# Two layers of cross attention and routed experts: the second attention's first batches prepared by groups, and new waits for gathers and scatters

## The chip, the cores and the metric

The kernel runs on one core of a Trainium2 chip. All data is float32. The metric is the device time of one execution in microseconds (us); the median of several executions is compared.

The core has five engines that run side by side, each with its own queue of instructions, worked off in order: TensorE (PE in the profile) multiplies matrices into PSUM banks, with its weight loads listed apart as PEld; VectorE (DVE) and ScalarE (ACT) work elementwise on SBUF and PSUM; GpSimd (POOL) works elementwise on SBUF and starts gathers and scatters by index; SyncE (SP) starts all other DMA transfers. An engine that needs another's result waits on a semaphore.

## The reference

The input x has 64 batches of 128 rows of 128 numbers. Each of two layers adds a cross attention and then a feed-forward part with two experts per row:

```python
x = x + xattn0(layernorm(x), fside, ctx, ctx)       # 16 heads of 8; keys: 128 made + 120 given
x = x + ffn0(layernorm(x))                          # each row: the best 2 of 8 experts, F = 352, gated
x = x + xattn1(layernorm(x), ctx, ctx)              # 16 heads of 8; 120 keys
x = x + ffn1(layernorm(x))                          # each row: the best 2 of 8 experts, R = 64, gelu
```

An attention is q = norm(x) Wq + bq, k = ctx Wk + bk, v = ctx Wv + bv, softmax(q k / sqrt(8)) v for each head, then Wo and bo. In ffn0 a row that chose experts e1 and e2 gets share1 * ffn(e1) + share2 * ffn(e2).

## The kernel before

The batches go in 16 groups of four (`GB = 4`); the rows of a group stay in SBUF in `xg[g]` from beginning to end. The kernel has three stages in time.

**First attention** (`attention(0, ...)`), with the first router inside it. The router chooses two experts for every row and scatters each row twice to the array `xs` in HBM, into places sorted by expert (L783, 128 scatters on GpSimd). Each scatter may overtake others, but is made to wait for the one four places before it (`DEEP = 4`, helper `behind`).

**Tile stage** (`tile_stage`): 71 tiles of 256 rows of one expert each. Tiles 0 to 31 (`NA = 32`) hold rows of the first ten groups' batches, the others the rest. Per tile: SyncE fetches rows, weights and shares (`fetch`, L1051, L1058), TensorE turns the rows (L1075), multiplies into the hidden layer (L1085, with ScalarE's L1089 and VectorE's L1090) and projects back (L1098); VectorE multiplies by the share (L1104) and SyncE writes 256 rows to the array `ys` in HBM (L1105). After tile t, `between(t)` runs some of the other work. A part of that is `first_results(t)`: for pairs of batches u = 0 to 3, starting at tile NA + 9 + 8u, in five steps at successive tiles: GpSimd gathers the rows of batches 2u and 2u + 1 from `ys` (four gathers, L1127), adds them to x (two additions, L1139), VectorE takes mean and variance (L112, L113), and after every second pair GpSimd makes the normed rows of a group (roots L155, rows L167, kept in `READY`) and adds a bias. So the normed rows of groups 0 and 1 are there when the stage ends. Keys and values of group 0 for the second attention are also made between tiles (L202, L214).

**Second attention** (`attention(1, ...)`, `first` false), with the second layer's feed-forward as `Aside1` inside it. Iteration `it` works on several batches at different steps. In the written order of one iteration: values of batch it - 3 (L446, copied by ScalarE L455); a round in which TensorE makes for batch `it` the products whose maximum VectorE takes (L373, L385), and for batch it - 2 the scores whose exponential ScalarE takes (L401, L409); a piece of the expert feed-forward; `prep(it, 0)`; the output steps of older batches (L475, L462, L482); router work; `prep(it, 1)`; `shift` for batch it - 1, which turns the maxima (L430) and adds them to the queries (VectorE L433).

Before a batch can take its L373 its queries must be there. For a whole group that is four steps: four turns of normed rows into one bank (`turned`, L176), one copy to SBUF `xnT` (ScalarE L177), one product with Wq 512 columns wide (L289), and four query pieces `q4` (ScalarE L293, each 512 wide). For group 0 the kernel before does it batch by batch instead (`prep_batch`): one turn (L313), one copy (L314), one product 128 wide (L316), four pieces 128 wide (L318), called once ahead of iteration 0 and then in iterations 0, 1 and 2. Group 1's four steps stand at the end of iteration 3 (L577 to L581), its keys (`prep_k`, L202, ScalarE L207) in iteration 1 and its values (`prep_v`, L214, VectorE L221) in iteration 2. Later groups are prepared by `prep`, spread over four iterations.

The order of TensorE, ScalarE, VectorE and GpSimd is that of the program text (`manual_schedule` with `ORDERED`); for SyncE a scheduler decides in most of the kernel. Waits are derived from what instructions read and write. Tiles come from pools: a tile of the same tag takes turns over `bufs` places, and a pool opened after another is closed takes over its memory. The second attention's work pool lies where the tile stage's had been, so the first users of its tiles wait for what used that memory: the tile stage's last instructions and its DMA transfers from or to it.

Two kinds of edits of waits occur in the code. `declare_no_dep(ins, group=...)` tells that an instruction doesn't conflict with those of a group, so no wait is derived between them. `behind(ins, earlier)` adds waits by hand. With them the gathers of `first_results` are declared free of the writes of tiles 32 on, and then put behind `needed`, the writes of tiles 32 to 39 + 8u.

Of the kernel before, what the change touches and what calls it, by code (L numbers as in the profile page):

```python
# [44 lines left out]
def transformer_kernel(ctx, tc, a, out):  # L45
# [186 lines left out]
    def attention(layer, w, norm, first, aside):  # L232
# [5 lines left out]
        with ExitStack() as es:  # L238
# [84 lines left out]
            def prep(it, half):  # L323

                g, j = it // GB + 1, it % GB
                if not first:
                    if g == 1:
                        if (j, half) == (2, 1):
                            prep_v(1)
                        elif (j, half) == (1, 0):  # L330
                            prep_k(1)
                    elif g < NG:
                        pieces = (
                            (), (lambda: prep_k(g),),
                            (lambda: prep_v(g), lambda: prep_x(g)),
                            (lambda: prep_q(g, 0), lambda: prep_q(g, 1)),
                        )[j]
                        if half < len(pieces):
                            pieces[half]()
# [172 lines left out]
            else:  # L512
                prep_batch(0)
                loads(1)
            oTs, pos_ = {}, {}

            for it in range(B + 5):
# [13 lines left out]
                if first and it % GB == 2:  # L531
                    norm_of(it // GB + 2)
                if 2 <= it <= B + 1:
                    ps_[it - 2] = work.tile([128, nc_, 4, 512], F32, name="p", tag="p")
# [23 lines left out]
                else:  # L558
# [4 lines left out]
                    aside.piece(mtile)  # L563
                    if it < GB - 1:
                        prep_batch(it + 1)
                    prep(it, 0)
# [8 lines left out]
                    if it > GB and it % GB == 1:  # L575
                        norm_of(it // GB + 1)
                    if it == GB - 1:  # L577
                        normed[1] = READY[1]
                        prep_x(1)
                        prep_q(1, 0)  # L580
                        prep_q(1, 1)  # L581
                    aside.fetch_for(it)
# [184 lines left out]

    AFTER = mybir.DependencyInfo(mybir.DependencyClass.Sync, mybir.DependencyReason.DATA)
    DEEP = 4
    scatters, spare = [], []  # L770

    def behind(ins, earlier):
        for e in earlier:
            tc.add_manual_dep(ins.ins, e.ins.name, AFTER, reason="rows of one array")

    def scatter(probe, j, k, xn):
# [9 lines left out]
        if scatters:  # L786
            tc.declare_no_dep(s.ins, group="scatters", reason="rows of their own")
        behind(s, [scatters[-DEEP] if len(scatters) >= DEEP else spare[0]])
        tc.add_to_no_dep_group("scatters", s.ins)
# [232 lines left out]
    def tile_stage(work, mtile):  # L1022
# [14 lines left out]
        def fetch(t):  # L1037
# [9 lines left out]
            share = s[:, n + 3 * TT : n + 3 * TT + 2].rearrange("p (h d) -> p h d", h=2)  # L1047
            first_ = scatters[2 * GA * GB - DEEP : 2 * GA * GB]
            assert len(first_) == DEEP
            for dst, src in ((x, xs[bass.ds(r, TT), :D]), (share, xs[bass.ds(r, TT), bass.ds(e + D, 1)])):  # L1050
                f = nc.sync.dma_start(dst, src.rearrange("(h p) d -> p h d", p=S))  # L1051
                if t < NA:

                    tc.declare_no_dep(f.ins, group="scatters", reason="rows of the first groups")
                    behind(f, first_)
                    tc.add_to_no_dep_group("scatters", f.ins)
# [56 lines left out]
        def first_results(t):  # L1113
# [6 lines left out]
            if step == 0:  # L1120
# [4 lines left out]
                for b in range(2):  # L1125
                    for k in range(2):
# [3 lines left out]
                        )  # L1130
                        tc.declare_no_dep(g.ins, group="writes", reason="other tiles")
                        behind(g, needed)
                        groups.add("reads")
# [172 lines left out]
    class Aside1:  # L1306


        def __init__(self, pool):
            self.pool, self.got, self.b, self.xn = pool, {}, 2 * GB, READY[0]  # L1310
            self.xnTs, self.gates, self.ready = {}, [], []
# [22 lines left out]
        def lead(self, b):  # L1334
# [7 lines left out]
            if b % GB == GB - 1:  # L1342
                norms[2].roots(b + 1 - GB, b + 1)

        def normed(self, j):

            return self.xn

# [183 lines left out]
```

## Time and profile before

| | |
|---|---|
| median of 3 runs | 1597.97 us (1597.46 to 1599.05) |
| the profiled execution | 1601.67 us |
| its span from first to last instruction | 1599.9 us |
| TensorE busy | 1484.9 us, 93% |
| VectorE busy | 1084.0 us, 68% |
| ScalarE busy | 843.9 us, 53% |
| GpSimd busy | 641.1 us, 40% |
| mean granted clock of TensorE | 0.959 of full |
| second attention begins | at about 988 us of the span |

A profile row of the timeline gives the start in the span, the duration, the engine, the line of the code, the operation, the tile written and the tiles read, shapes, and a count where several equal instructions are put together. In brackets stands how long the engine had been idle before and what ended the wait. A float32 product appears as two matmul instructions (L289, one product, is "x2"), a turn (L176, L313) as one. A row of the table of windows gives for a stretch of time how busy each engine was, then the clock that TensorE was granted (1.00 is full speed), the share in which DMA engines were busy, and GB/s moved. The chain of work is followed back from the last instruction through what each waited for.

### The profile page before, as it was taken

To read this page: it belongs to the slowest core of one execution; us is meant where nothing else is said; L and a number is where in the kernel's file an instruction comes from. 1 tells how busy PE (TensorE), PEld (TensorE's weight loads), DVE (VectorE), ACT (ScalarE), POOL (GpSimd) and SP (SyncE) were. 2 spreads that over 40 slices of the span, in tenths; PEclk is the share of its full clock that TensorE was granted. 3 is DMA by queue.
4 is the path that set the end of the run, shared out by engine and by line. 5 is a ranking of instruction groups with operands and counts; after the bars stand their busy time and mean duration, and the time that the engine had idled before them with its cause. 6 is when DMAs were issued, how large, how long until landed. Compare 5 with 4: busy or idle time off the path is not lost.

```text
span 1599.9 us, 45004 instructions
## 1 busy us (share of the span) xinstructions
PE 1484.9 (93%) x18162; PEld 1182.0 (74%) x18162; DVE 1084.0 (68%) x2960; ACT 843.9 (53%) x1739; POOL 641.1 (40%) x1195
## 2 busy tenths in 40 slices
PE   7989999999999999888999998988999999999987
PEld 5767777777777777777888887767777777777765
DVE  6757888888888986454744443677666666667753
ACT  4646666666666655432333333666555555555643
POOL 4122255555565535443020302366554544443210
PEclk9999999999999999999999999799999989999999
DMA  8842122222222221466776664110111100000000
GB/s 218 228 115 59 48 57 56 62 60 60 60 60 59 53 71 44 133 190 186 202 212 193 201 186 127 30 32 21 37 31 29 31 29 28 27 27 15 15 8 27
DMA packets 143586, 133.22 MB, mean 83 GB/s; under 512 B 48402, under 2 KB 125970, under 8 KB 141458
## 3 DMA queue, kind: packets, MB, share of 16 engines
q1 hardware_dynamic: 135186, 113.02, 25.7%
q0 software_dynamic: 8192, 17.32, 3.5%
q8 instruction: 144, 2.36, 0.6%
q14 instruction: 64, 0.52, 0.1%
HBM read 97.31 MB, written 32.97 MB: 81 GB/s over the span
## 4 chain that ended last, share of the span: by engine, by line
PE 73%; DVE 10%; DMA 4%; issue 3%; SPq 3%; POOL 3%; ACT 3%; another core or an unknown queue 0%; POOLq 0%; ACTq 0%; DVEq 0%
PE bank L401 12%; PE bank L373 12%; PE bank L446 9%; PE bank L1085 9%; PE bank L1413 4%; PE bank L1392 4%; PE bank L1098 3%; DVE nm L385 3%; PE bank L289 2%; SPq L1247 2%; PE bank L1402 2%; PE bank L482 2%; DMA q<-xs 2%; PE bank L214 2%; PE bank L652 2%
## 5 line engine op out<-in xcount | busy, mean ns | idle before, releaser
L385 DVE TENSOR_REDUCE nm<-bank 128x2 f32<-128x496 f32 (+1 forms) x768 | 465.9, 664 | 141.3 <-PE bank L401 69.5
L401 PE MATMUL bank<-q,k 32*120 32x256 f32 (+1 forms) x3072 | 478.0, 408 | 16.4 <-DVE nm L385 5.0
L409 ACT ACTIVATE p<-bank 120x512 f32<-120x512 f32 (+1 forms) x768 | 403.3, 605 | 140.5 <-PE bank L401 106.0
L373 PE MATMUL bank<-k,q 32*128 32x248 f32 (+1 forms) x4096 | 462.4, 345 | 13.3 <-DMA k<-in_ctx_k 7.1
L373 PEld LDWEIGHTS bank<-k,q 32*128 32x128 f32 x4096 | 351.8, 191 | 81.6 <-issue 36.3
L401 PEld LDWEIGHTS bank<-q,k 32*120 32x120 f32 (+1 forms) x3072 | 302.0, 182 | 45.9 <-DVE nm L385 16.0
L446 PE MATMUL bank<-p,v 128*32 128x128 f32 (+1 forms) x4096 | 179.3, 279 | 4.6 <-DVE nm L385 3.9
L1090 DVE TENSOR_TENSOR p<-p,bank 128x256 f32<-128x256 f32 x213 | 87.8, 420 | 125.3 <-ACT p L1089 106.9
L155 POOL TENSOR_SCALAR rstd<-mv 128x4 f32<-128x4 f32 x32 | 6.3, 198 | 384.9 <-DVE mv L113 296.4
L783 POOL DMA_INDIRECT xs<-xn,at x128 | 129.4, 1011 | 28.5 <-issue 24.9
L455 ACT COPY ov<-bank 128x256 f32<-128x256 f32 x128 | 47.9, 375 | 170.5 <-PE bank L446 141.3
L1089 ACT ACTIVATE p<-bank 128x256 f32<-128x256 f32 x213 | 80.8, 385 | 102.4 <-PE bank L1085 92.4
L446 PEld LDWEIGHTS bank<-p,v 128*32 128x32 f32 (+1 forms) x4096 | 111.4, 111 | 29.6 <-issue 13.0
L1085 PE MATMUL bank<-q 128*128 128x256 f32 x516 | 122.4, 388 | 4.4 <-ACT oT L477 4.4
L433 DVE SCALAR_TENSOR_TENSOR q<-bank,c_smask,q 128x256 f32<-128x256 f32 x256 | 111.4, 477 | 12.7 <-PE bank L430 11.9
L1328 POOL DMA_INDIRECT yb<-ys,back x112 | 108.8, 971 | 27.7 <-issue 20.1
L167 POOL TENSOR_SCALAR xn<-x,mv,rstd 128x128 f32<-128x128 f32 x252 | 110.2, 447 | 7.5 <-issue 1.4
L293 ACT ACTIVATE q<-bank,c_a_bq,c_hmask 128x512 f32<-128x512 f32 x120 | 87.4, 787 | 45.3 <-PE bank L289 45.2
L1085 PEld LDWEIGHTS bank<-q 128*128 128x128 f32 x516 | 97.5, 196 | 17.0 <-ACT oT L477 4.8
L446 PE MATMUL bank<-p,vc 120*32 120x128 f32 x2048 | 104.2, 272 | 0.6 <-issue 0.5
L138 POOL TENSOR_TENSOR mv<-st 128x4 f32<-128x4 f32 x31 | 6.4, 206 | 205.4 <-DVE st L109 205.4
L1085 PE MATMUL bank<-vc 128*128 128x256 f32 x336 | 77.2, 379 | 0.0
(220 smaller groups left out, 2364.5 us busy)
## 6 DMA issues: line engine op xcount, KB each, us to landing
q<-in_w SPq DMA_DIRECT2D x43, 576.0 KB
vc<-in_w SPq DMA_DIRECT2D x28, 576.0 KB
vc<-in_ctx_v SPq DMA_DIRECT2D x16, 960.0 KB
ys<-zero SPq DMA_DIRECT2D x71, 128.0 KB
k<-in_ctx_k SPq DMA_DIRECT2D x32, 240.0 KB
q<-xs SPq DMA_DIRECT2D x43, 128.0 KB
ys<-q SPq DMA_DIRECT2D x43, 128.0 KB
x<-in_x SPq DMA_DIRECT2D x16, 256.0 KB
```

The costliest lines, as they stand in the source:

```text
L167: nc.gpsimd.tensor_scalar(xn[:, j, :D], xg[g][:, j, :], self.mv[:, b, 0:1], self.rstd[:, b : b + 1], ALU.add, ALU.mult,)
L293: nc.scalar.activation(q4s[g][:, :, s, :], pq.rearrange("p (b q) -> p b q", b=GB), AF.Identity, bias=w["bq"][:, s : s + 1], scale=hmask[:, ...
L373: nc.tensor.matmul(pa[:, u, :], lhsT=q4s[g][r, j, s, :], rhs=k2[g % 2][r, s // 2, j, :], start=True, stop=True,)
L385: nc.vector.tensor_reduce(nm[b % 2].rearrange("q i (a s) -> q a i s", s=16)[:, 2 * ra + v : 2 * ra + v + len(slots) // 2, :, 0], pa.rearra ...
L401: nc.tensor.matmul(pb[:n, v * 256 : (v + 1) * 256], lhsT=k2[g % 2][r, v, j, k0 : k0 + n], rhs=q4s[g][r, j, 2 * v : 2 * v + 2, :].rearrange ...
L409: nc.scalar.activation(ps_[b][:n, c, ra, :], pb[:n], AF.Exp, scale=SCALE)
L433: nc.vector.scalar_tensor_tensor(q, pm, smask[:, v : v + 1], q, ALU.mult, ALU.add)
L446: nc.tensor.matmul(pav[32 * ra : 32 * ra + 32, v * S : (v + 1) * S], lhsT=vs[g % 2][c][:, j, 4 * v + ra, i, :], rhs=p[:n, c, ra, (2 * v + ...
L783: s = nc.gpsimd.indirect_dma_start(xs, bass.IndirectOffsetOnAxis(at[:, j, k : k + 1], 0), xn, None)
L1085: nc.tensor.matmul(ph[:, u, :], lhsT=w[:, c, u * 128 : (u + 1) * 128], rhs=xT, start=True, stop=True)
L1090: nc.vector.tensor_tensor(hT[:, c, :], sa, ph[:, 1, :], ALU.mult)
L1328: nc.gpsimd.indirect_dma_start(y[:, k, b % 2, :], None, ys, bass.IndirectOffsetOnAxis(back[:, b, k : k + 1], 0),)
```

## The change

The second attention begins by groups: before iteration 0 the four steps run for all of group 0 (`prep_x(0)`, `prep_q(0, 0)`, `prep_q(0, 1)`), and `prep_batch` is no longer called. Group 1's keys, values and turn move to iteration 0, its product and query pieces to iteration 1. The first tile of `p` is asked for ahead of `xnT`, so `xnT` lies in other memory than before, where `p`'s first tile had been. Scatters, the first tiles' fetches and the gathers in `first_results` no longer get their waits from `behind`, but name in `keep=` the instructions of the group which they still wait for: a scatter the one four before it, a fetch all eighty scatters of the first groups (instead of the last four of them), and a gather the writes of tiles 32 to 39 + 8u. In the built program the waits that differ within the tile stage are those of the gathers: before, they don't wait for these writes, after, they do.

```diff
--- before.py
+++ after.py
@@ -325,10 +325,13 @@
                 g, j = it // GB + 1, it % GB
                 if not first:
                     if g == 1:
-                        if (j, half) == (2, 1):
+                        if (j, half) == (0, 0):
+                            prep_k(1)
                             prep_v(1)
-                        elif (j, half) == (1, 0):
-                            prep_k(1)
+                        elif (j, half) == (0, 1):
+                            prep_x(1)
+                        elif j == 1:
+                            prep_q(1, half)
                     elif g < NG:
                         pieces = (
                             (), (lambda: prep_k(g),),
@@ -510,8 +513,14 @@
                 prep_batch(0)
                 yield
             else:
-                prep_batch(0)
+
+                ps_[0] = work.tile([128, nc_, 4, 512], F32, name="p", tag="p")
                 loads(1)
+                for g in range(2):
+                    normed[g] = READY[g]
+                prep_x(0)
+                prep_q(0, 0)
+                prep_q(0, 1)
             oTs, pos_ = {}, {}
 
             for it in range(B + 5):
@@ -530,7 +539,7 @@
 
                 if first and it % GB == 2:
                     norm_of(it // GB + 2)
-                if 2 <= it <= B + 1:
+                if 2 <= it <= B + 1 and it - 2 not in ps_:
                     ps_[it - 2] = work.tile([128, nc_, 4, 512], F32, name="p", tag="p")
                 if it % GB == 0 and 0 < it // GB + 1 < NG:
                     if it:
@@ -561,8 +570,6 @@
 
 
                     aside.piece(mtile)
-                    if it < GB - 1:
-                        prep_batch(it + 1)
                     prep(it, 0)
                     on(4, out3)
                     on(3, out2)
@@ -574,11 +581,6 @@
                     aside.ahead(it)
                     if it > GB and it % GB == 1:
                         norm_of(it // GB + 1)
-                    if it == GB - 1:
-                        normed[1] = READY[1]
-                        prep_x(1)
-                        prep_q(1, 0)
-                        prep_q(1, 1)
                     aside.fetch_for(it)
                     aside.call(it, mtile)
                 ps_.pop(it - 3, None)
@@ -765,13 +767,8 @@
     nc.vector.memset(zero, 0.0)
     filled = []
 
-    AFTER = mybir.DependencyInfo(mybir.DependencyClass.Sync, mybir.DependencyReason.DATA)
     DEEP = 4
     scatters, spare = [], []
-
-    def behind(ins, earlier):
-        for e in earlier:
-            tc.add_manual_dep(ins.ins, e.ins.name, AFTER, reason="rows of one array")
 
     def scatter(probe, j, k, xn):
 
@@ -784,8 +781,10 @@
             xs, bass.IndirectOffsetOnAxis(at[:, j, k : k + 1], 0), xn, None
         )
         if scatters:
-            tc.declare_no_dep(s.ins, group="scatters", reason="rows of their own")
-        behind(s, [scatters[-DEEP] if len(scatters) >= DEEP else spare[0]])
+            tc.declare_no_dep(
+                s.ins, group="scatters", keep=[scatters[-DEEP].ins] if len(scatters) >= DEEP else [],
+                reason="rows of their own",
+            )
         tc.add_to_no_dep_group("scatters", s.ins)
         scatters.append(s)
 
@@ -1045,14 +1044,16 @@
             x, y = (s[:, n + TT * k : n + TT * (k + 1)].rearrange("p (h d) -> p h d", h=2) for k in range(2))
             xT_of[t] = s[:, n + 2 * TT : n + 3 * TT]
             share = s[:, n + 3 * TT : n + 3 * TT + 2].rearrange("p (h d) -> p h d", h=2)
-            first_ = scatters[2 * GA * GB - DEEP : 2 * GA * GB]
-            assert len(first_) == DEEP
+            first_ = scatters[: 2 * GA * GB]
+            assert len(first_) == 2 * GA * GB
             for dst, src in ((x, xs[bass.ds(r, TT), :D]), (share, xs[bass.ds(r, TT), bass.ds(e + D, 1)])):
                 f = nc.sync.dma_start(dst, src.rearrange("(h p) d -> p h d", p=S))
                 if t < NA:
 
-                    tc.declare_no_dep(f.ins, group="scatters", reason="rows of the first groups")
-                    behind(f, first_)
+                    tc.declare_no_dep(
+                        f.ins, group="scatters", keep=[s.ins for s in first_],
+                        reason="rows of the first groups",
+                    )
                     tc.add_to_no_dep_group("scatters", f.ins)
                 if dst is x:
                     nc.sync.dma_start(
@@ -1128,8 +1129,9 @@
                             y[:, k, b, :], None, ys,
                             bass.IndirectOffsetOnAxis(back[:, 2 * u + b, k : k + 1], 0),
                         )
-                        tc.declare_no_dep(g.ins, group="writes", reason="other tiles")
-                        behind(g, needed)
+                        tc.declare_no_dep(
+                            g.ins, group="writes", keep=[w.ins for w in needed], reason="other tiles"
+                        )
                         groups.add("reads")
                         tc.add_to_no_dep_group("reads", g.ins)
             elif step == 1:
@@ -1307,7 +1309,7 @@
 
 
         def __init__(self, pool):
-            self.pool, self.got, self.b, self.xn = pool, {}, 2 * GB, READY[0]
+            self.pool, self.got, self.b = pool, {}, 2 * GB
             self.xnTs, self.gates, self.ready = {}, [], []
             for k in range(2):
                 t = pool.tile([S, QM, 32], F32, name=f"gates_{k}", tag=f"gates_{k}")
@@ -1341,10 +1343,6 @@
             norms[2].stats(b)
             if b % GB == GB - 1:
                 norms[2].roots(b + 1 - GB, b + 1)
-
-        def normed(self, j):
-
-            return self.xn
 
         def made(self, b):
             norms[3].stats(b)
```

## The prediction

> **What bounds the kernel now.** I read the page's chain of work first, then the slices with TensorE's granted clock, then the timeline and the table of windows where the two layers meet, since that is where most of the edits lie.
>
> ```profile
> PE 1484.9 (93%) x18162; PEld 1182.0 (74%) x18162; DVE 1084.0 (68%) x2960; ACT 843.9 (53%) x1739; POOL 641.1 (40%) x1195
> ...
> PE 73%; DVE 10%; DMA 4%; issue 3%; SPq 3%; POOL 3%; ACT 3%; another core or an unknown queue 0%; POOLq 0%; ACTq 0%; DVEq 0%
> ```
>
> TensorE sets the time, so an edit counts by what it does to TensorE's queue. Behind the second attention's beginning its queue is the same instruction for instruction in both programs, so a shift there reaches the end. The beginning in the timeline (start, duration, engine, line, tile; in brackets the idle time before and who ended it):
>
> ```profile
> 988.24 0.30 PE L313 MATMUL bank<-ident,xn 128*128 128x128 f32 x1 [0.79 <-DVE q L1104]
> 990.63 0.27 ACT L314 COPY xnT<-bank 128x128 f32<-128x128 f32 x1 [5.43 <-DMA ys<-q]
> 990.95 0.49 PE L316 MATMUL bank<-xnT,c_a_wq 128*128 128x128 f32 x2 [2.40 <-ACT xnT L314]
> 991.47 1.51 ACT L318 ACTIVATE q<-bank,c_a_bq,c_hmask 128x128 f32<-128x128 f32 x4 [0.58 <-PE bank L316]
> 991.99 3.38 PE L373 MATMUL bank<-k,q 32*128 32x120 f32 x32 [0.55 <-ACT q L318]
> ...
> 1003.78 1.81 PE L202 MATMUL bank<-kvT,c_a_wk 128*128 128x480 f32 x2
> ...
> 1012.50 1.91 PE L214 MATMUL bank<-c_a_wv,kvT 128*120 128x128 f32 x8
> ...
> 1019.33 0.60 PE L176 MATMUL bank<-ident,xn 128*128 128x128 f32 x4
> 1020.02 0.59 ACT L177 COPY xnT<-bank 128x512 f32<-128x512 f32 x1
> 1020.66 1.12 PE L289 MATMUL bank<-xnT,c_a_wq 128*128 128x512 f32 x2 [0.73 <-ACT xnT L177]
> 1021.83 2.79 ACT L293 ACTIVATE q<-bank,c_a_bq,c_hmask 128x512 f32<-128x512 f32 x4 [1.22 <-PE bank L289]
> ```
>
> Two things are to be seen: each batch 0 to 3 pays turn, copy, product and query pieces in a row before its L373, and everything waits from 988.54 to 990.63 for the tile stage's last write. The windows show a third, the clock (the last columns are granted clock, DMA share and GB/s):
>
> ```profile
> core 0: us, PE busy (x) PEld busy (x) DVE busy (x) ACT busy (x) POOL busy (x), PEclk, DMA share, GB/s
> 992.56:995.97 3.41, 3.21 (x31) 2.71 (x29) 1.83 (x3) 0.42 (x2) 2.80 (x3) 0.50 0.30 101
> ...
> 1006.21:1009.62 3.41, 3.41 (x40) 3.34 (x44) 2.48 (x6) 2.96 (x5) 1.57 (x2) 0.50 0.14 41
> 1009.62:1013.04 3.42, 2.65 (x21) 1.99 (x18) 1.22 (x2) 1.76 (x5) 0.00 (x0) 0.50 0.00 0
> 1013.04:1016.45 3.41, 3.41 (x41) 2.79 (x39) 1.92 (x6) 1.22 (x4) 0.00 (x0) 0.50 0.26 71
> 1016.45:1019.86 3.41, 3.41 (x64) 2.90 (x56) 2.09 (x4) 2.38 (x5) 0.00 (x0) 1.00 0.02 6
> ```
>
> TensorE runs at half clock from 992.56 to 1016.45.
>
> **The change, part by part.**
>
> *Batch by batch to by groups.* Removed from TensorE: four L313 with four L316; from ScalarE: four L314 (0.27) and four fours of L318 (1.51). Added: one group's turn (L176 0.60, L177 0.59, L289 1.12, L293 2.79). Group 1's same four steps, which stood behind iteration 3 (rows 1019.33 to 1021.83), move to iteration 0 and 1; with them L202 from iteration 1 and L214 from iteration 2 to iteration 0, and their bias additions on ScalarE and VectorE (L207 1.40, L221). SP's and POOL's orders are unchanged. Walking forward from 988.24:
>
> 1. L176 ends at 988.84. The copy still starts at 990.63 (below), so 991.22; L289 to 992.39 at full clock; L293 to about 995.2.
> 2. L373 of batch 0 is paced by L293: its last 12 products, 0.21 each at half clock (3.38/16), follow 995.2, so it ends at 997.8, where before it ended at 995.37: **2.4 later**.
> 3. L202 (1.81) and L214 (1.91) at half clock: 1001.5. Their context, issued by SP at 990.27, has had 7.5 us. Then L176 at half clock, 1.2: 1002.7.
> 4. That is 4.9 us of products over the whole array in one stretch. Before, nothing like it occurs until 1013.04, when the rest of L214 (1.4), L430 (0.6) and L446 follow one another, and that window brings the clock back. So I take it to be back at 1002.8, not 1016.45.
> 5. L373 of batch 1 at full clock, 1.7: 1004.4. L289 1.12, L430 0.38: 1005.9. Round of iteration 2: 2.24, as before's at 1016.58 to 1018.82 (at half clock 4.65, 1005.94 to 1010.6): about 1009.0 with the gap for L433 (0.88).
> 6. ScalarE is now behind: L293 of group 1 ends at 1008.3, the exponentials' table load (1.28) at 1009.6, four exponentials at 1011.9. So L446 of batch 0 starts at 1011 to 1012, before 1014.77: **about 3.3 earlier**.
> 7. TensorE idles in 1009.6 to 1013.0 meanwhile. If the clock stays full, L446 of batch 1 follows at 1016.4, before 1021.72: 5.3 earlier. If it falls again, at 1018.8 (2.9 earlier), and some 0.3 more goes in that window's sequel. I take the middle, (5.3 + 2.6)/2 = **4.0 earlier**. A fall is as likely as not, since the window holds round, L430 and idling in about the mix of 995.97 to 999.38.
>
> *What the clock rule would make of it.* The window row 1006.21 to 1009.62 has TensorE busy 3.41 of 3.41 and the clock still at 0.50 after it. The Trainium skill, "TensorE: Matmul & The Clock Gate", Part 1, says full clock follows about 3.4 us of sustained busy. By that, before's 3.21 in the first half-clock window, or 3.41 in the fifth, should have ended it, and there would be little half clock for the change to shorten: then three chains of some 1.7 (copy 0.27, product 0.49, first query piece 0.38, gaps 0.3 and 0.3) go, 5.2, against a beginning longer by 2.6 (batch 0's L373 at full clock would end at 995.2 + 12 x 0.106 = 996.5, before at about 993.9): 2.6 earlier. The trace disagrees with the rule as soon as busy is made of L373 and L401, which use 32 of 128 rows; products of the whole array did bring the clock back. I follow the row, 4.0; the rule's 2.6 is inside the range.
>
> *Turned rows in other memory.* xnT now lies where the first tile of p lay. That memory too is of the pool that the tile stage used, and its release still waits for the last ys write (issued 988.12, seen at 990.42 and 990.63 by POOL and ScalarE) in the built program. Zero. Were it free, the copy could start at 988.9: 1.7 more gain. SP's load at 990.27 wouldn't come sooner.
>
> *Gathers wait for their tiles.* This is the only wait changed in the tile stage. Before, the first four gathers run at 817.82, long before tile 39's write:
>
> ```profile
> 817.82 1.00 POOL L1127 DMA_INDIRECT kvT<-ys,back  x1 [80.92 <-DVE p L1090]
> 825.41 0.72 POOL L1139 TENSOR_TENSOR x<-x,kvT 128x256 f32<-128x256 f32 x1 [1.30 <-DMA kvT<-ys,back]
> ```
>
> Now pair u waits for the writes of tiles up to 39, 47, 55 and 63, issued by SP at 851.77, 887.61, 923.51 and 960.73. Behind the gather on POOL stand only the two additions, then roots, normed rows and bias; POOL has tens of us to spare. VectorE's L112 needs the sums, and behind it wait L1104 and L1090, so the tiles. A write takes 2.3 (988.12 to 990.42), four gathers and additions 8.3 (817.82 to 826.13; 8.9 in the next pair, 826.41 to 835.28): done at about 862.3, 898.7, 934.1 and 971.5. L112 stands at 865.14, 900.57, 938.09, 973.81: **slack 2.8, 1.9, 4.0 and 2.3**. Cost zero while it lasts; beyond it each microsecond of lateness is a microsecond of tile stage. Gathers at other times meet the same tile fetches (the slices show 190 to 210 GB/s at 817 as at the later ones), so above all u=1 might spill by 0 to 1. The edits to scatters and fetches change no wait on either queue.
>
> **The sum.** 4.0 less in the profiled execution: 1601.67 becomes 1597.7. That execution is 3.7 above the median of the timed runs, 1597.97, so I carry the difference over: **1594.0**. What a measurement tells from no change, 0.2%, is 3.2 us.
>
> **Rivals.**
>
> - *The clock comes back no sooner in effect (about −1, 1597).* The windows lie on a grid that the kernel doesn't set. If before, in most executions, regains full clock at an L214 or L202 earlier than in this trace, or after falls back at 1013 for two windows, half of the 4.0 goes and the longer start (2.4) stays. For it: thin work in 1009.6 to 1013. Against: 4.9 us in one stretch always puts at least 2.4 of it into one window.
> - *Half clock lasts on, slower (1600.7).* The place is steps 4 to 7: if the 4.9 us stretch isn't enough, ScalarE's L293 and the table load keep TensorE's work thin, and no L214 follows later in iterations 2 and 3 to lift it. A round then costs 4.65 in place of 2.24: L446 of batch 1 at 1024.4, 2.7 late. It decides from 1020 on: each further half-clock round adds 2.4, so one more gives 5.1 late, one fewer nothing. Against: L176 and L289 of later groups are full-array work too.
> - *Gathers overrun (1601.0 and more).* If landing takes 4.5 longer than at 817, the four pairs are late by 1.7, 2.6, 0.5 and 2.2, seven in sum, against the 4.0 gained. Against: POOL's rows above show 1.30 to 2.3 of waiting for landing in all.
> - *The memory does free the copy (1592.3).* The change then does more than I read in the waits.
>
> **How the numbers follow.** Steps as above 0.62 (1591.5 to 1597; two thirds of it below 1594.8, so 0.42 faster, 0.20 the same); clock no sooner 0.12 (same); half clock lasts 0.12 (0.08 slower, 0.04 same); gathers 0.09 (0.08 slower, 0.01 same); copy freed 0.05 (faster). Faster 0.47, same 0.37, slower 0.16. The range 1590.3 to 1601.0 leaves out some 0.05 below (clock held and copy freed together) and 0.15 above.
>
> **What would show it.** Right: L177 at 990.6 behind the ys write; half clock ending some ten microseconds sooner after 988 than before; L446 of batch 1 at 28 to 31 us past the last tile's products where it was 33.5; L112 behind L1104 without idle in the tile stage. Wrong: VectorE's idle ended by POOL's x in front of L112; clock at 0.50 past 1020; the copy at 988.9.

## The result

The changed kernel takes 1592.49 us in the median of 12 runs (1589.10 to 1598.65), the kernel before 1599.07 us in 12 runs on the same chip (1595.85 to 1607.19). The ratio is 0.9954 (95% interval 0.9934 to 0.9974): 0.46% faster, 7.4 us by the ratio, 6.6 us by the medians. The forecast was 4.0 us.

The profile after, first the page (lines of the code are shifted by 1 to 3: L373 is now L376, L401 is L404, L409 is L412, L430 is L433, L446 is L449):

```profile
span 1587.5 us, 44979 instructions
...
PE 1472.8 (93%) x18156; PEld 1169.8 (74%) x18156; DVE 1081.6 (68%) x2960; ACT 839.0 (53%) x1724; POOL 640.5 (40%) x1195
...
PE 71%; DVE 11%; DMA 5%; SPq 3%; ACT 3%; issue 3%; POOL 3%; another core or an unknown queue 0%; POOLq 0%; ACTq 0%; DVEq 0%
```

TensorE still sets the time. The beginning of the second attention in the timeline (start, duration, engine, line, tile):

```profile
989.05 0.63 PE L176 MATMUL bank<-ident,xn 128*128 128x128 f32 x4 [0.79 <-DVE q L1105]
991.43 0.59 ACT L177 COPY xnT<-bank 128x512 f32<-128x512 f32 x1 [5.43 <-DMA ys<-q]
992.07 1.12 PE L289 MATMUL bank<-xnT,c_a_wq 128*128 128x512 f32 x2 [2.39 <-ACT xnT L177]
993.23 2.79 ACT L293 ACTIVATE q<-bank,c_a_bq,c_hmask 128x512 f32<-128x512 f32 x4 [1.22 <-PE bank L289]
994.06 4.24 PE L376 MATMUL bank<-k,q 32*128 32x120 f32 x32 [0.87 <-ACT q L293]
...
998.23 1.97 PE L202 MATMUL bank<-kvT,c_a_wk 128*128 128x480 f32 x2
...
1000.00 1.91 PE L214 MATMUL bank<-c_a_wv,kvT 128*120 128x128 f32 x8
...
1001.70 1.06 PE L176 MATMUL bank<-ident,xn 128*128 128x128 f32 x4
...
1002.69 2.24 PE L376 MATMUL bank<-k,q 32*128 32x120 f32 x32
...
1006.02 2.79 ACT L293 ACTIVATE q<-bank,c_a_bq,c_hmask 128x512 f32<-128x512 f32 x4 [2.58 <-PE bank L289]
...
1008.83 1.28 ACT L412 ACT_TABLE_LOAD   x1
```

The copy to xnT still starts when the last ys write is seen, so the other memory frees nothing. The query pieces pace the first L376, and the stretch L202, L214, L176 stands where it was put. The table of windows shows the clock (third number from the right):

```profile
993.40:996.82 3.42, 2.76 (x21) 2.41 (x24) 0.00 (x0) 2.62 (x4) 2.79 (x3) 0.50 0.32 97
996.82:1000.23 3.41, 3.41 (x22) 2.26 (x16) 2.45 (x4) 0.00 (x0) 1.53 (x3) 0.50 0.09 24
1000.23:1003.64 3.41, 3.41 (x20) 3.08 (x20) 0.75 (x2) 1.98 (x3) 2.77 (x3) 0.50 0.25 64
1003.64:1007.06 3.42, 3.19 (x36) 2.20 (x32) 2.02 (x4) 1.04 (x2) 2.25 (x3) 1.00 0.25 85
1007.06:1010.47 3.41, 2.53 (x46) 2.14 (x46) 3.13 (x8) 3.38 (x5) 2.05 (x3) 1.00 0.12 36
1010.47:1013.88 3.41, 2.10 (x49) 1.59 (x49) 2.13 (x6) 2.09 (x5) 0.00 (x0) 1.00 0.04 10
```

Half clock lasts three windows, 10.2 us, where it lasted seven, 23.9. To compare kernels I count from the first turn of group 0 behind the last tile (988.24 before, 989.05 here) to VectorE's first maximum of batch 4, and call that **the beginning**:

```profile
1025.18 1.22 DVE L385 TENSOR_REDUCE nm<-bank 128x4 f32<-128x480 f32 x2 [3.37 <-PE bank L373]
```

```profile
1018.81 1.22 DVE L388 TENSOR_REDUCE nm<-bank 128x4 f32<-128x480 f32 x2 [0.34 <-PE bank L376]
```

It lasts 36.9 us before, 29.8 after, 7.2 less. That is about the measured gain of 6.6 to 7.4. In the two profiled executions the span differs by more, 12.4 us: the program behind that point took 574.7 us before and 568.7 after, with 71.7 and 61.7 us of half clock in it (from 60 us behind the first turn on). When the changed kernel was profiled again, on chip C below, it had 72.0 us of half clock there and took 576.2 us; and on chip A the kernels with and without the grouping both took 518 us there (518.2 and 518.1). So I put the 6 us behind that point down to the one execution, not to the change.

The gathers (POOL) and the statistics that need them (DVE), second pair:

```profile
891.67 0.96 POOL L1128 DMA_INDIRECT kvT<-ys,back  x1 [27.88 <-issue]
...
898.67 1.53 POOL L1141 TENSOR_TENSOR x<-x,kvT 128x256 f32<-128x256 f32 x2 [2.28 <-DMA kvT<-ys,back]
```

```profile
901.16 0.61 DVE L1105 TENSOR_SCALAR q<-bank,q 128x128 f32<-128x128 f32 x2 [0.50 <-PE bank L1099]
901.68 0.28 DVE L112 BATCH_NORM_STATS2 st<-x 128x6 f32<-128x128 f32 x1
```

The sums end at 900.20, 1.5 us ahead of L112, which has no bracket: it didn't wait. For the four pairs the sums end 1.3, 1.5, 1.7 and 3.2 us ahead.

### The profile page after: what moved, and what is told of

It is laid out like the page before. It is cut to its first block, busy times and chain, and to the rows that moved or that the text cites. A ratio compares the mean times of both kernels' runs of the same rounds, so it can differ in the third digit from the quotient of the medians.

```text
span 1587.5 us, 44979 instructions
## 1 busy us (share of the span) xinstructions
PE 1472.8 (93%) x18156; PEld 1169.8 (74%) x18156; DVE 1081.6 (68%) x2960; ACT 839.0 (53%) x1724; POOL 640.5 (40%) x1195
## 4 chain that ended last, share of the span: by engine, by line
PE 71%; DVE 11%; DMA 5%; SPq 3%; ACT 3%; issue 3%; POOL 3%; another core or an unknown queue 0%; POOLq 0%; ACTq 0%; DVEq 0%
PE bank L404 12%; PE bank L376 12%; PE bank L449 9%; PE bank L1086 8%; PE bank L1411 4%; PE bank L1390 4%; PE bank L1099 3%; DVE nm L388 3%; DMA q<-xs 3%; PE bank L289 2%; SPq L1249 2%; PE bank L1400 2%; PE bank L485 2%; PE bank L214 2%; PE bank L202 2%
## 5 line engine op out<-in xcount | busy, mean ns | idle before, releaser
L404 PE MATMUL bank<-q,k 32*120 32x256 f32 (+1 forms) x3072 | 474.0, 406 | 13.1 <-DVE nm L388 5.0
L412 ACT ACTIVATE p<-bank 120x512 f32<-120x512 f32 (+1 forms) x768 | 402.4, 603 | 142.6 <-PE bank L404 119.0
L376 PE MATMUL bank<-k,q 32*128 32x248 f32 (+1 forms) x4096 | 459.7, 342 | 16.7 <-DMA k<-in_ctx_k 11.5
L376 PEld LDWEIGHTS bank<-k,q 32*128 32x128 f32 x4096 | 348.9, 188 | 84.2 <-issue 37.2
L404 PEld LDWEIGHTS bank<-q,k 32*120 32x120 f32 (+1 forms) x3072 | 299.3, 180 | 45.1 <-DVE nm L388 16.0
L449 PE MATMUL bank<-p,v 128*32 128x128 f32 (+1 forms) x4096 | 178.3, 276 | 5.0 <-DVE nm L388 2.8
L1090 ACT ACTIVATE p<-bank 128x256 f32<-128x256 f32 x213 | 80.9, 384 | 101.0 <-PE bank L1086 90.8
L449 PEld LDWEIGHTS bank<-p,v 128*32 128x32 f32 (+1 forms) x4096 | 110.0, 109 | 29.3 <-issue 13.0
L449 PE MATMUL bank<-p,vc 120*32 120x128 f32 x2048 | 103.9, 272 | 0.5 <-issue 0.5
L1128 POOL DMA_INDIRECT kvT<-ys,back x16 | 15.4, 961 | 194.9 <-DMA vc<-xs 117.3
```

The lines of the kernel that those rows point to most:

```text
L376: nc.tensor.matmul(pa[:, u, :], lhsT=q4s[g][r, j, s, :], rhs=k2[g % 2][r, s // 2, j, :], start=True, stop=True,)
L404: nc.tensor.matmul(pb[:n, v * 256 : (v + 1) * 256], lhsT=k2[g % 2][r, v, j, k0 : k0 + n], rhs=q4s[g][r, j, 2 * v : 2 * v + 2, :].rearrange ...
L412: nc.scalar.activation(ps_[b][:n, c, ra, :], pb[:n], AF.Exp, scale=SCALE)
L449: nc.tensor.matmul(pav[32 * ra : 32 * ra + 32, v * S : (v + 1) * S], lhsT=vs[g % 2][c][:, j, 4 * v + ra, i, :], rhs=p[:n, c, ra, (2 * v + ...
```

## The experiments

The experiments ran on three chips, A, B and C, on each beside runs of the kernel before. The chips differ: the kernel before took 1527.09 us (median) on A, 1611.01 on B, 1612.97 on C. So times are compared as ratios on one chip, and profiles by the beginning. The full change ran on the chip of the result above and on C, not on A or B; the kernel before has one profile, the one ahead of the prediction.

| kernel | ratio to before (95% interval) | the beginning, us | half clock in it, us |
|---|---|---|---|
| chip A | | | |
| grouping alone | 0.9966 (0.9954 to 0.9979) | 31.3 | 10.2, then 3.4 |
| waits alone | 1.0005 (0.9988 to 1.0023) | 36.7 | 27.3 |
| group 1's keys and values late | 0.9950 (0.9925 to 0.9976) | 30.2 | 13.6 |
| group 0 alone | 0.9949 (0.9931 to 0.9967) | 28.9 | 13.6 |
| chip B | | | |
| added products, after | 0.9960 (0.9938 to 0.9982) | 28.5 | 6.8, from 17 on |
| added products, before | 0.9999 (0.9987 to 1.0011) | 34.0 | 0 |
| gathers one tile later | 0.9982 (0.9970 to 0.9993) | 29.8 | 10.2 |
| group 0 alone, early copy, added products | 0.9950 (0.9932 to 0.9969) | 28.5 | 10.2, from 8 on |
| chip C | | | |
| the full change again | 0.9961 (0.9947 to 0.9975) | 31.6 | 10.2, then 6.8 |
| group 0 alone, again | 0.9966 (0.9951 to 0.9981) | 32.4 | 20.5 |
| group 1's queries later | 0.9963 (0.9949 to 0.9976) | 31.6 | 10.2, then 6.8 |
| the same as the last of chip B, clock held | 0.9946 (0.9931 to 0.9962) | 28.4 | 0 |

### Which half of the change it is

Grouping alone (the kernel before with the edits of the second attention, `behind` and its waits kept):

> The kernel before with the grouped beginning alone; gathers, scatters and fetches keep their old waits. Measure of the beginning: from the first turn of group 0 behind the last tile to VectorE's first maximum of batch 4, 37.0 us in the profile before, 29.7 after. Theory (the grouping is the whole gain): beginning 29.7, half clock for three windows (10.2 us) in it, time 5 to 8 us below the kernel before, as the full change. Rival (part of the gain comes from the gathers' new places in the tile stage): beginning 29.7 all the same, but only 3 to 4 us below before.

Waits alone (the changed kernel with the attention of before):

> The kernel before with the edits of gathers, scatters and fetches alone; the beginning stays batch by batch. Theory: beginning 37.0, tile stage unchanged to 0.5 us, VectorE's batch statistics find the sums 1 to 3 us early, time within 1.5 us of the kernel before. Rival (the gathers' new places help the tile stage): 2 to 4 us below. Other rival (they overrun in some executions): above.

The grouping alone gives 0.34% (0.21 to 0.46), 5.2 us of 1527, and a beginning 5.4 us shorter than in the kernel with the waits alone (31.3 against 36.7). The waits alone give 0.05% the other way, with no change inside the interval. So the gain is the grouping's as far as it can be told: the interval of the full change (0.9934 to 0.9974, on another chip) overlaps with the grouping's. In time the first theory holds in both; the beginning of the grouping alone was expected at 29.7 and came at 31.3, with a second fall of the clock.

The new waits of the gathers are worth something else than time. In the kernel before, the first gathers start at 817.82, 34 us ahead of the issue of tile 39's write at 851.77, though its text names this write among those they need; in the changed kernel they start at 855.14, behind it. What the early gathers read is not shown here.

### What the early keys, values and queries of group 1 are worth

Keys and values late:

```diff
-                        if (j, half) == (0, 0):
-                            prep_k(1)
-                            prep_v(1)
-                        elif (j, half) == (0, 1):
+                        if (j, half) == (2, 1):
+                            prep_v(1)
+                        elif (j, half) == (1, 0):
+                            prep_k(1)
+                        if (j, half) == (0, 1):
                             prep_x(1)
```

> The full change, but keys and values of group 1 are made in iterations 1 and 2 again, where the kernel before makes them; the turn and queries of group 1 stay early. Theory (the stretch of full-array products L202, L214, L176 brings the clock back): without L202 and L214 the stretch is 1.1 us, full clock comes back a window or more later than after (half clock 13.7 to 24 us instead of 10.2), beginning 31 to 35 us. Rival (shorter chains are all that matters, the clock follows PE's busy time alone): half clock 10.2, beginning 29 to 30.5.

Group 0 alone: `prep_k(1)` and `prep_v(1)` as above, and the turn and queries of group 1 back at the end of iteration 3:

```diff
+                    if it == GB - 1:
+                        prep_x(1)
+                        prep_q(1, 0)
+                        prep_q(1, 1)
```

> The full change, but all of group 1's work (keys, values, turn, queries) stands where the kernel before has it; only group 0 is prepared as a group. Theory (chains worth about 2.6, the earlier clock the rest): half clock lasts as in the kernel before or one window less, 20 to 24 us, beginning 33 to 36. Rival (the chains alone carry the gain): beginning 29.5 to 31.

> Only group 0 prepared as a group, group 1's work where the kernel before has it, again, beside the full change. Theory (in the full change group 1's query pieces stand ahead of the exponentials' table load on ScalarE and hold batch 0's values up, some 2.5 us): batch 4 at 28.5 to 29.5, batch 0's values (first product of L446) at 19 to 20 instead of 22.6, time 1.5 to 3 us below the full change. Rival (it comes out even once the pipeline is full): within 1 us of the full change.

The windows of group 0 alone, chip A:

```profile
974.60:978.00 3.40, 2.53 (x15) 1.92 (x18) 0.00 (x0) 2.79 (x4) 2.48 (x4) 0.50 0.45 140
978.00:981.40 3.40, 3.40 (x52) 3.40 (x53) 2.76 (x5) 0.00 (x0) 1.12 (x2) 0.50 0.12 28
981.40:984.80 3.40, 3.40 (x12) 1.82 (x10) 2.30 (x5) 0.85 (x2) 2.63 (x3) 0.50 0.07 19
984.80:988.20 3.40, 3.40 (x43) 3.33 (x45) 2.23 (x6) 2.92 (x4) 2.52 (x3) 0.50 0.24 60
988.20:991.60 3.40, 3.40 (x71) 2.85 (x67) 2.98 (x8) 1.46 (x3) 2.44 (x4) 1.00 0.20 47
```

In time none of the three differs from the early work clear of noise: on A 0.9950 and 0.9949 against 0.9966 for the grouping, on C 0.9966 against 0.9961 for the full change. Both theories of the moved work were half right. On the clock mine: the five kernels with the whole stretch early that hold no added products (after, grouping alone, gathers one tile later, the full change again, queries later) have full clock back after three windows each time, 10.2 us; with keys and values late it took 13.6, with group 0 alone 13.6 and 20.5. On the time the rival: an early return isn't needed for the gain. In two of the table's kernels with the stretch the clock also fell a second time behind it, for 6.8 us, in a third for 3.4.

The windows above also contradict the reason I gave for the clock. 984.80 to 988.20 holds a round of L373 and L401 with no break (its first product starts at 984.27), and full clock follows. In the kernel before the same round from 1006.21 to 1009.62, as busy, was not followed by it. So a window that holds nothing but products on 32 rows can be the last one ahead of full clock. In the same table two windows as busy, 978.00 and 981.40, were followed by half clock. What decides between these windows stays open.

### What ScalarE's order costs

My step 6 had group 1's query pieces hold up the exponentials. Queries later:

```diff
-                        elif j == 1:
+                        elif j == 2:
                             prep_q(1, half)
```

> The full change, but group 1's product with Wq and its query pieces stand in iteration 2 instead of 1, behind that round's exponentials on ScalarE; keys, values and turn stay early. Theory (it is the query pieces ahead of the table load that cost): batch 0's values at 19.5 to 21 instead of 22.6, most of the distance to the kernel with group 0 alone. Rival (what costs is the product work of group 1 on TensorE ahead of batch 0's scores): values at 22 to 23 as in the full change.

Batch 0's values (first product of L449) came at 24.6 us, later than the full change's 22.6 to 22.7, with half clock from 17.7 on and L289, now in iteration 2, directly ahead of them (2.08 us at half clock); batch 4 at 31.6 as in the full change again. Neither theory had that place, and there is no gain in time (0.9963 against 0.9961). That the query pieces stand ahead of the table load is seen in the profile, 1006.02 to 1008.83 then the load; that it costs the kernel anything is not shown. On A group 0 alone had its values at 19.3, on C at 22.8 with 20.5 us of half clock, so there the rival held: the advantage of one profile was gone in the next.

### Clock or chains

Four products in the waits of the changed beginning (512 wide, on the whole array, results unused; two behind group 0's turn and two behind its product with Wq):

```diff
+                def fill(n):
+                    pf = mtile()
+                    xn = READY[1].rearrange("q b d -> q (b d)")
+                    for _ in range(n):
+                        nc.tensor.matmul(pf, lhsT=w["wq"], rhs=xn, start=True, stop=True)
+
                 prep_x(0)
+                fill(2)
                 prep_q(0, 0)
                 prep_q(0, 1)
+                fill(2)
```

> The full change, with four added products (512 wide, whole array, result unused) where TensorE waits at the beginning: two between group 0's turn and its product with Wq, two behind that product while ScalarE makes the query pieces; 1.12 us each at full clock, in idle time of 2.4 and about 3 us. Theory (half clock at the beginning costs 2 to 4 us even after the change): half clock in the beginning 0 to 3.4 us instead of 10 to 14, first maximum of batch 4 at 26 to 28 us behind the first turn, 2 to 4 us below the full change. Rival (the beginning is set by ScalarE's query pieces, table load and exponentials, not by TensorE's clock): clock full but batch 4 at 29 to 30.

The same kind of products in the batch-by-batch beginning, in `prep_batch` behind the turn (512 wide, two for batch 0) and behind the product with Wq (256 wide):

> The kernel before, batch by batch, with added products (whole array, result unused) in TensorE's waits: behind each turn 512 wide (two for batch 0), behind each product with Wq 256 wide. It holds the clock up and leaves the four chains as they are. Theory (of the 7 us by which the beginning got shorter, more than half is clock, the rest the chains): clock full from the start or after one window, batch 4 at 28.5 to 31 us where the kernel before has 37, time 5 to 8 below the kernel before. Rival (chains alone): batch 4 at 35 to 37 though the clock is full.

In the kernel before with added products the clock is full through the whole beginning, and the time is that of the kernel before (0.9999, 0.9987 to 1.0011):

```profile
994.21:1028.24 34.03, 27.69 (x302) 18.90 (x303) 14.78 (x33) 17.66 (x38) 13.08 (x16) 1.00 0.17 47
```

TensorE's rows in it (here L373 is L385, L313 is L320, L316 is L326, the added products L306):

```profile
997.96 2.31 PE L385 MATMUL bank<-k,q 32*128 32x120 f32 x32
1000.21 0.33 PE L320 MATMUL bank<-ident,xn 128*128 128x128 f32 x1
1000.37 1.02 PE L306 MATMUL bank<-xn,c_a_wq 128*128 128x512 f32 x2
1003.22 0.49 PE L326 MATMUL bank<-xnT,c_a_wq 128*128 128x128 f32 x2 [1.83 <-ACT xnT L321]
1003.55 0.60 PE L306 MATMUL bank<-xn,c_a_wq 128*128 128x256 f32 x2
1004.26 2.31 PE L385 MATMUL bank<-k,q 32*128 32x120 f32 x32
```

From the products of batch 0 to those of batch 1 it is 6.30 us (997.96 to 1004.26) at full clock; in the kernel before it was 6.48 (991.99 to 998.47) at half clock. But the added product may stand in the chain: ScalarE's copy starts 2.37 us behind the turn's recorded end here (1000.54 to 1002.91) and 1.04 before (995.77 to 996.81):

```profile
995.30 0.47 PE L313 MATMUL bank<-ident,xn 128*128 128x128 f32 x1
996.81 0.27 ACT L314 COPY xnT<-bank 128x128 f32<-128x128 f32 x1 [3.82 <-PE bank L313]
```

So some of the 6.30 can be the experiment's own, and what this chain takes at full clock is not known. Compare group 0 prepared as a group, on C, where batch 1's products follow batch 0's at once, both at half clock:

```profile
1002.38 6.28 PE L374 MATMUL bank<-k,q 32*128 32x120 f32 x64 [0.87 <-ACT q L294]
1002.38:1008.66 6.28, 6.28 (x65) 5.72 (x65) 3.38 (x6) 1.96 (x3) 4.49 (x6) 0.50 0.17 44
```

Two batches in 6.28 us, 3.14 each. So the chain between batches 0 and 1 costs about 3.3 us at half clock (6.48 less 3.14). The change removes three such chains, but not three times 3.3. In that profile of group 0 alone half clock lasts nearly as long as in the kernel before (20.5 and 23.9 us), and the distances between the first maxima of batches 0 to 3 shrink by 4.2, 0.6 and 2.8 us, 7.7 in all; batch 0's comes 3.1 later. (At batch 2 TensorE now waits 1.03 us for VectorE's shifted queries.) That leaves 4.6 of the 7.2 us, on two chips, and this kernel has 0.34% of the full change's 0.39% in time, on one. So the chains are the larger part of the gain. How much the clock adds is not settled: in the profiles the full clock shortened the batch-by-batch beginning from 36.9 to 34.0 us (two chips), and the time shows none of it.

For the changed kernel the added products gave 0.9960 (0.9938 to 0.9982), the same as without, with full clock for 17 us and then 6.8 us of half clock, and batch 4 at 28.5. My expectation of 2 to 4 us more was not met, nor was the rival's clock.

### The early copy, and a version that holds the clock

Group 0 alone, with its xnT in a tile of the router's pool, and three added products (one behind the turn, two behind the product with Wq); then the same with one more behind the maxima of batch 0 and of batch 1. Of the edits, that of xnT:

```diff
             def prep_x(g):
-                xnT = work.tile([D, GB * S], F32, name="xnT", tag="xnT", bufs=1)
+                if g == 0 and not first:
+                    xnT = rp.tile([D, GB * S], F32, name="xnT", tag="xnT", bufs=1)
+                else:
+                    xnT = work.tile([D, GB * S], F32, name="xnT", tag="xnT", bufs=1)
```

> Group 0 prepared as a group, group 1's work where the kernel before has it; its xnT in memory of the router, which no late write touches, so the copy needn't wait for the last tile's write; and three added products (unused) to hold the clock. Theory (chains, clock and that wait add up): copy 1.7 us earlier, query pieces then wait for the write, start 1.5 earlier; batch 4 at 25 to 27 us, time 9 to 12 below the kernel before. Rival (the clock falls later instead, or ScalarE is the bound): batch 4 at 28 to 29, 7 to 8 below.

> Group 0 alone as a group, xnT in memory that no late write touches, three added products in the waits ahead of batch 0 and one more behind each of the first two batches' maxima (0.9 us each, result unused), to keep the clock from falling at 8 us as it did with the three alone. Theory (the early copy's 2 us were eaten by half clock from 8 us on): clock full, batch 4 at 25 to 27, time 9 to 12 below the kernel before. Rival (the added products cost what the clock gives): batch 4 at 28 to 29.5.

The copy does start early in this memory, 0.7 us behind the turn's start instead of 2.4:

```profile
997.33 0.63 PE L176 MATMUL bank<-ident,xn 128*128 128x128 f32 x4 [0.79 <-DVE q L1117]
...
998.03 0.58 ACT L177 COPY xnT<-bank 128x512 f32<-128x512 f32 x1 [3.76 <-PE bank L176]
...
999.89 2.78 ACT L296 ACTIVATE q<-bank,c_a_bq,c_hmask 128x512 f32<-128x512 f32 x4 [1.27 <-PE bank L292]
```

The first maximum then comes at 5.9 us instead of 7.5 to 8.8. With three products the clock fell at 8 us for 10.2 and batch 4 came at 28.5; with five it stayed full, and batch 4 still came at 28.4:

```profile
991.72:1020.13 28.41, 25.45 (x288) 17.34 (x289) 14.20 (x33) 14.34 (x23) 13.09 (x16) 1.00 0.20 55
```

So of the 2 us won at the first maximum little is left at batch 4, and holding the clock won nothing there. The numbers are those of the rival in both expectations; that the added products cost what the clock gave is not shown. In time the version with the clock held is 0.9946 (0.9931 to 0.9962), 8.7 us below the kernel before, the lowest on chip C; beside the full change's 0.9961 (0.9947 to 0.9975) that is 2.4 us, and the intervals overlap. It is ahead of the kernel before clear of noise, ahead of the change not.

### How near the gathers are

```diff
-                needed = written[NA : NA + E * (u + 1)]
+                needed = written[NA : NA + E * (u + 1) + 1]
```

> The full change, but each pair of gathers waits for one tile more (40, 48, 56, 64), some 4.6 us later; nothing else. In the profile after the sums stand 1.3, 1.5, 1.7 and 3.2 us ahead of VectorE's statistics. Theory (no slack is left behind that, and lateness holds the tiles up one for one): VectorE waits 3.3, 3.1, 2.9 and 1.4, tile stage about 8 to 11 us longer, time 3 us above to 3 us below the kernel before. Rival (the tile stage has slack of its own, being bound by fetches): tile stage within 3 us, time as the full change.

VectorE's row for the second pair:

```profile
913.58 0.29 DVE L112 BATCH_NORM_STATS2 st<-x 128x6 f32<-128x128 f32 x1 [3.15 <-POOL x L1141]
```

L112 now waits 2.5, 3.2, 2.3 and 2.9 us, 10.8 in all, and the tile stage is 346.0 us long instead of 336.8 (from its first to its last L1090): 9.2 more, but on another chip. In the profiles on B and C of kernels that don't touch this wait the stage lasted 337 to 342 us (346.6 once), so the waits' share of the 9.2 is not known. The ratio is 0.9982, 2.9 us below the kernel before, at the edge of what the theory had. Beside 0.9954 to 0.9961 for the full change, on other chips, that is a loss of 0.2 to 0.3%, some 3 to 5 us; but the interval overlaps with that of the full change with added products on B (0.9938 to 0.9982). The waits as written have 1.3 us to spare at the tightest pair; one tile later VectorE already waits for the sums.

## Why the prediction was right

The direction, the class (faster by more than 0.2%) and the range hold; the time lies 1.5 us below the forecast. By its steps, counted from the first turn:

| step | forecast | profile after |
|---|---|---|
| 1: L289 ends; query pieces end | 4.2; 7.0 | 4.1; 7.0 |
| 2: L373 of batch 0 ends | 9.6 | 9.3 |
| 3: group 1's L176 ends | 14.5 | 13.7 |
| 4: full clock back | 14.6 | 14.6 |
| 5: round of iteration 2 ends | 20.8 | 21.0 |
| 6: L446 of batch 0 starts | 22.8 to 23.8 | 22.7 |
| 7: L446 of batch 1 starts | 28.2 (clock holds), 30.6 (falls again) | 27.1; on chip C: 28.9 (fell again) |

The row of step 7, before and after:

```profile
1021.72 1.08 PE L446 MATMUL bank<-p,v 120*32 120x128 f32 x32
```

```profile
1016.13 1.56 PE L449 MATMUL bank<-p,v 120*32 120x128 f32 x32
```

The mis-sized term is step 7. The forecast took 4.0 us as the middle of 5.3 and 2.6. Batch 1's values came 6.4 us earlier where the clock held (33.5 to 27.1) and 4.6 where it fell again (28.9). The two differ by 1.8 us, not by 2.7, and both lie below what the forecast had for their case. By batch 4 another 0.8 is won where the clock held (7.2). A fall "as likely as not" fits: three of the five kernels with the stretch early and nothing added show one.

The walk came true step by step, but the weight it gave to the early clock did not. Steps 4 to 7 draw the gain from full clock at 1002.8; group 0 alone, without the early stretch and with half clock for 13.6 and 20.5 us, is as fast within noise. That the range held is therefore in part luck: the chains alone, 2.6 us by its own sum, gave 4.6 in the profile of group 0 alone, and what the clock added is not settled.

The alternative that followed the clock rule gave 2.6, from chains of 1.7 us that it summed from durations, 5.2 for three. It failed on the size of the chain: 3.3 us between batches 0 and 1, and 7.7 for the three in group 0 alone. Its sum left out the turn and the wait for its result, 1.5 us in the rows above (995.30 to 996.81). On the rule itself (the Trainium skill, "TensorE: Matmul & The Clock Gate", Part 1) both sides have a row now: 1006.21 to 1009.62 before, fully busy without full clock after it, and 984.80 to 988.20 of group 0 alone with it. Whole-array products in the waits did keep the clock full throughout, in the kernel before with added products and in the last version.

The gathers cost nothing, as forecast, but the slack was thinner in three of four pairs: 1.3, 1.5, 1.7 and 3.2 us against 2.8, 1.9, 4.0 and 2.3. The first gathers of the four pairs started 3.4 us (851.76 to 855.14), 3.3, 2.1 and 2.1 behind their write's issue, not 2.3 as the last write of the stage suggested. The rival of overrunning gathers named the right place: it is a tile away. The other memory frees nothing, as forecast. Of the rivals, "half clock lasts on" didn't come; "clock back no sooner" nearly came in group 0 alone on chip C (20.5 us of half clock against 23.9), without taking the gain away. Of the signs named, batch 1's values missed theirs (27.1 us, not 28 to 31) on the good side.

## What to carry to other kernels

When a pipeline starts, price the chain between two batches by the distance from one batch's products to the next, not by the sum of its instructions' durations: here 3.3 us against 1.7 for the first pair of batches. Don't multiply it: for three chains 7.7 us came off, not 10. Prepare the first few batches together if only the first of them then starts later (2.2 us here, by its first maximum), and look at that before the clock. Where a wait is moved into a running stage, find the instruction that needs its result and how early the result is there: 1.3 us was enough, a tile more was not.

## What the runs showed of the hardware

The same code took 1527 us on one chip and 1599 to 1613 on others. In the profile of the kernel with the waits alone, on the first (A), the program from 60 us behind the first turn on held 7.1 us of half clock; the kernel before, on its chip, 71.7. In all it is 65.2 against 129.7, and TensorE's busy time 1433.7 against 1484.9 us. Why the chips differ was not tried.

Two executions of one kernel, here on two chips, can also differ by several microseconds at the start of a stage: group 0 alone had 13.6 us of half clock in one profile and 20.5 in the other, and its beginning took 28.9 and 32.4 us. A profile of each of two kernels is not enough to rank them at 0.2%; the ratios were needed.
